# Spreading the next item's first matmuls over the current item's seams, and the routing over the next item's layer 0

## The chip, the cores and the metric

The kernel runs on one core of a Trainium2 chip, with eight items (a batch of 8) worked through one after the other in a single launch. The metric is the device time of one launch in microseconds; the kernel before takes 2810.74 us (median of 3 runs, 2806.79 to 2811.39). The engines are named as the profile names them: PE is TensorE's matmul, PEld its weight load, DVE is VectorE, ACT is ScalarE, POOL is GpSimd, SP is SyncE.

## What is computed

All is fp32. Each item is an image of 256 channels and 1024 positions (tokens). Cut to what matters:

```python
# layer 0: eight heads of width 64, softmax over the QUERY axis
qkv  = xt @ w_qkv + b_qkv
attn = softmax(einsum('bihd,bjhd->bijh', q, k) * SCALE, axis=1)
x    = einsum('bijh,bjhd->bihd', attn, v) @ w_out + b_out + xt
# layer 1
n1 = layer_norm(x)
t  = x + softmax((n1 @ W.T) @ n1.T) @ n1
n2 = layer_norm(t)
# 8 experts, the best 2 per token
probs   = softmax(n2 @ router_w.T)
combine = top 2 of probs, divided by their sum
moe     = n2 + sum over e of combine[:, e] * (gelu(n2 @ w1[e] + b1[e]) @ w2[e] + b2[e])
out     = t + moe
```

## The kernel before

The first seven items go through layer 0, attention and routing; the routing scatters their normalised tokens to memory by expert. The last item's layer 0 is followed by all blocks of the experts, and the last item itself takes all experts in a dense way. One item on the way, in the order of the program:

```python
for b in range(B):
    xT = next_x
    if b + 1 < B:
        next_x = load_x(b + 1)
    t1 = layer0(b, xT)
    if b + 1 < B:
        t2 = attend(b, t1)
        dispatch(b, t2, groups[0])
        continue
    ...   # last item: experts, then attend and dense
```

Layer 0 begins with the values for all heads and the first pair of heads' q and k. `big` is a PSUM tile of 1024 columns, of which there are three buffers; `acc` one of 512 columns, of which there are two, both held by the output `po` all through layer 0.

```python
def project(b, xT, g, t):                      # q (t=0) or k (t=1) of one pair of heads
    pq = big(f"pqk_{b}_{g}_{t}")
    ...                                        # 4 matmuls of 512 columns
    dst = two.tile([P, S], F32, tag=f"qk{t}", ...)
    evicted[b, g, t] = nc.vector.tensor_scalar(dst, pq, b_qk[...], ..., ALU.add, ALU.mult)
    return dst

def values(b, xT):
    v = one.tile([P, NT, INNER], F32, tag="v", name=f"v_{b}")
    for i in range(0, NT, 2):                  # 4 parts of two token blocks
        pv = big(f"pv_{b}_{i}")
        ...                                    # 4 matmuls of 512 columns
        for j in range(2):
            nc.vector.tensor_add(v[:, i + j, :], pv[:, ts(j, 512)], b_v)
    return v

def layer0(b, xT):
    v = values(b, xT)
    res = one.tile([P, NPAIR, S], F32, tag="res", name=f"res_{b}")
    qks = [[project(b, xT, 0, t) for t in range(2)]]
    if b == 0:
        prepare()
    steps = [(g, j) for g in range(NPAIR) for j in range(NT)]    # 4 pairs x 8 blocks
    ...
    for at in range(last + LAG + 1):
        if at <= last:
            score(at, 0, 0)                    # psc: scores, a big buffer per head
        if 0 < at <= last + 1:
            score(at - 1, 1, 1)
            soften(at - 1, 1)                  # DVE maximum, ACT exponential; DVE scales v
        if at <= last:
            first_max(at, 0)                   # DVE maximum of the first half
            score(at, 0, 1)
            score(at, 1, 0)
            soften(at, 0)
            first_max(at, 1)
        if at >= LAG:
            gather_values(at - LAG)            # po: exponentials times values
        if at <= last:
            g, j = steps[at]
            if g + 1 < NPAIR and j in (3, 5):
                ...
                qks[g + 1].append(project(b, xT, g + 1, len(qks[g + 1])))
    ...                                        # pr: output projection and residual into t1
```

Attention normalises, transposes (`pt`, copied to nT), multiplies with W (`px`, copied to xa), and takes the eight blocks of queries in turn, scores of one block ahead of the products of the one before:

```python
def attend(b, t1, step=lambda i: None):
    n1 = one.tile([P, NT, D], F32, tag="n", name=f"n1_{b}")
    layer_norm(t1, n1, 1e-5, f"a{b}")
    nT = ...
    to_channels(n1, nT, f"n1_{b}")             # 16 transposes on PE, two copies on DVE
    ...                                        # px, xa
    def mix(i, ex, ssum):
        pt = big(f"pa_{b}_{i}")
        for m in range(NT):
            nc.tensor.transpose(pt[:, ts(m, P)], ex[:, ts(m, P)], ident)
        aT = two.tile([P, S], F32, tag="tr", name=f"aT_{b}_{i}")
        nc.vector.tensor_copy(aT, pt)
        py = acc(f"py_{b}_{i}")
        ...                                    # 8 matmuls, then rs and the sum into t2
```

`dispatch` then does the second norm, the transposes, the logits on TensorE (`pl`), and the routing, a chain of small VectorE instructions of 64 or 8 elements per partition: gates (softmax and the two largest), then the row of every token in its expert's list (with two small matmuls, `pc` and `pn`, that count over the partitions), then 16 indirect DMAs:

```python
def dispatch(b, t2, group):
    n2 = one.tile([P, NT, D], F32, tag="n", name=f"n2_{b}")
    layer_norm(t2, n2, 1e-5, f"f{b}")
    nT = ...
    to_channels(n2, nT, f"n2_{b}")
    gate, hots = gates(b, nT)                  # pl on PE, then the gates on DVE
    ...
    pc = acc(f"pc_{b}")
    nc.tensor.matmul(pc[:, : NT * E], before, flat, start=True, stop=True)
    pn = acc(f"pn_{b}")
    nc.tensor.matmul(pn[:, : NT * E], ones, flat, start=True, stop=True)
    ...                                        # rows, counts, and per choice: row, exp, at
    for i in range(NT):
        for k in range(2):
            nc.gpsimd.indirect_dma_start(out=view[:, :], ..., in_=n2[:, i, :], in_offset=None)
    nc.gpsimd.tensor_add(t2, t2, n2)
    nc.sync.dma_start(group.sums[group.items.index(b)], t2)
```

The order of the program is not wholly that of an engine: the compiler's scheduler may bring a ready instruction forward when an earlier one waits, as far as buffers are free. Buffers of one kind are given out in the program's order.

Of the kernel before, what the change touches and what calls it, by code (L numbers as in the profile page):

```python
# [10 lines left out]
F32 = mybir.dt.float32  # L11
I32 = mybir.dt.int32
AF = mybir.ActivationFunctionType
ALU = mybir.AluOpType
# [4 lines left out]
def kernel(  # L19
# [266 lines left out]
    def values(b, xT):  # L286
        v = one.tile([P, NT, INNER], F32, tag="v", name=f"v_{b}")
        for i in range(0, NT, 2):
            pv = big(f"pv_{b}_{i}")
            for j in range(2):  # L290
                for cc in range(NCC):
                    nc.tensor.matmul(  # L292
                        pv[:, ts(j, 512)],
                        xT[:, cc, ts(i + j, P)],
# [4 lines left out]
            for j in range(2):  # L299
                nc.vector.tensor_add(v[:, i + j, :], pv[:, ts(j, 512)], b_v)  # L300
        return v

    def layer0(b, xT):
# [4 lines left out]
        v = values(b, xT)  # L308
        res = one.tile([P, NPAIR, S], F32, tag="res", name=f"res_{b}")
        qks = [[project(b, xT, 0, t) for t in range(2)]]  # L310
        if b == 0:
            prepare()
# [81 lines left out]
        for at in range(last + LAG + 1):  # L394
# [13 lines left out]
# [3 lines that stand above are left out]
                    if j == 3:  # L411
                        qks.append([])
                    qks[g + 1].append(project(b, xT, g + 1, len(qks[g + 1])))

# [16 lines left out]
    def attend(b, t1, step=lambda i: None):  # L431
        n1 = one.tile([P, NT, D], F32, tag="n", name=f"n1_{b}")
        layer_norm(t1, n1, 1e-5, f"a{b}")
        nT = one.tile([P, NCC, S], F32, tag="nT", name=f"nT_{b}")
# [35 lines left out]
        def mix(i, ex, ssum):  # L470
            pt = big(f"pa_{b}_{i}")
# [3 lines left out]
            nc.vector.tensor_copy(aT, pt)  # L475
            py = acc(f"py_{b}_{i}")
# [22 lines left out]
    def gates(b, nT):  # L499

        pl = acc(f"pl_{b}")
        for i in range(NT):
            for dc in range(NCC):
# [6 lines left out]
                )  # L510

# [6 lines left out]
        pl3 = pl[:, : NT * E].rearrange("p (i e) -> p i e", e=E)  # L518
        m = col("g_m")
        nc.vector.tensor_reduce(m, pl3, AX.X, ALU.max)  # L520
        p = tmp("g_p")
        nc.vector.tensor_sub(p, pl3, bcast(m, E))
        nc.scalar.activation(p, p, AF.Exp)
        z = col("g_z")
        nc.vector.tensor_reduce(z, p, AX.X, ALU.add)
        nc.vector.reciprocal(z, z)
        nc.vector.tensor_mul(p, p, bcast(z, E))

        def first_of_max(src, tag):
# [3 lines left out]
            nc.vector.tensor_tensor(hot, src, bcast(top, E), ALU.is_equal)  # L533
            nc.vector.tensor_mul(hot, hot, rank)
# [4 lines left out]
        top1, hot1 = first_of_max(p, "g_1")  # L539
        rest = tmp("g_rest")  # L540
        nc.vector.scalar_tensor_tensor(rest, hot1, -2.0, p, ALU.mult, ALU.add)
        top2, hot2 = first_of_max(rest, "g_2")
# [25 lines left out]
    def dispatch(b, t2, group):  # L568

        n2 = one.tile([P, NT, D], F32, tag="n", name=f"n2_{b}")  # L570
        layer_norm(t2, n2, 1e-5, f"f{b}")
        nT = one.tile([P, NCC, S], F32, tag="nT", name=f"n2T_{b}")
        to_channels(n2, nT, f"n2_{b}")
        gate, hots = gates(b, nT)
# [7 lines left out]
        pc = acc(f"pc_{b}")  # L582
        flat = both.rearrange("p i e -> p (i e)")
        nc.tensor.matmul(pc[:, : NT * E], before, flat, start=True, stop=True)
        pn = acc(f"pn_{b}")
# [11 lines left out]
        )  # L597
        rows = tmp("d_rows")
# [474 lines left out]
```

## Time and profile before

| what | number |
|---|---|
| time, median of 3 | 2810.74 us |
| span of the profiled execution | 2745.2 us |
| TensorE busy | 2617.9 us (95%) |
| VectorE busy | 1539.6 us (56%) |
| ScalarE busy | 841.2 us (31%) |
| mean granted TensorE clock | 0.983 |
| q, k projections, 512 matmul records | 233.9 us |
| values, 256 matmul records | 137.5 us |

Busy times overlap, so they don't add up to the span. One fp32 matmul of the program stands as two records in the trace; records are pipelined, and a record can begin before the one ahead of it ends, so the mean of a record can be longer than the distance from one to the next. A line of waits reads: engine, tile and line that waited, what it waited for, total us, number of times, the longest. A line of a table by stage reads: stretch, its length, then for PE, PEld, DVE, ACT and POOL the busy us and the number of instructions, then the granted clock, the DMA's busy share, and GB/s.

### The profile page before, as it was taken

What the parts mean: (1) busy time and instruction counts of PE and PEld (TensorE: products, weight loads), DVE (VectorE), ACT (ScalarE), POOL (GpSimd) and SP (SyncE); (2) the same over time, 40 slices, a digit from 0 to 9 for tenths busy, and PEclk for the clock granted to TensorE, in tenths of its full rate; (3) what the DMA queues carried; (4) which work ended last, traced back from release to release, by engine and by line L of the source; (5) the groups of instructions that cost most, each with busy time, mean ns of one, the idle gap of its engine ahead of it and who ended that gap; (6) DMA issues with size and microseconds to landing.
All of it is one profiled execution on the core that took longest, in us unless ns stands there. A gap on an engine that the chain in (4) does not pass through costs nothing.

```text
span 2745.2 us, 27697 instructions
## 1 busy us (share of the span) xinstructions
PE 2617.9 (95%) x10153; PEld 1378.9 (50%) x10153; DVE 1539.6 (56%) x3667; ACT 841.2 (31%) x1455; POOL 385.7 (14%) x383
## 2 busy tenths in 40 slices
PE   8999899989999999999999999899989999999899
PEld 3345433653356335633464346433653377776566
DVE  4764566456744665466645764566456753334544
ACT  2441155114521443134312541145114521111122
POOL 0000200020000200020002000200020024444652
PEclk9999999999999999999999999999999999999999
DMA  6992100000000000010001000100010135553542
GB/s 232 385 340 47 62 1 1 16 35 12 1 16 16 31 1 16 10 37 1 16 0 46 1 1 16 46 1 1 0 37 10 41 125 180 180 178 103 177 141 97
DMA packets 82512, 182.37 MB, mean 66 GB/s; under 512 B 15016, under 2 KB 24904, under 8 KB 80584
## 3 DMA queue, kind: packets, MB, share of 16 engines
q1 hardware_dynamic: 57368, 118.65, 12.1%
q0 software_dynamic: 25008, 61.95, 7.3%
q8 instruction: 80, 1.31, 0.2%
q14 instruction: 56, 0.46, 0.1%
HBM read 100.49 MB, written 110.90 MB: 77 GB/s over the span
## 4 chain that ended last, share of the span: by engine, by line
PE 83%; issue 8%; DVE 4%; ACT 3%; DMA 0%; POOL 0%; ACTq 0%; SPq 0%; DVEq 0%
PE psc L324 20%; PE po L382 17%; PE pqk L273 8%; PE py L478 8%; PE ps L456 7%; PE pv L292 5%; PE pr L420 4%; PE px L441 2%; PE pdh L950 2%; PE pdy L974 2%; PE pt_n L218 2%; PE pa L473 2%; PE pe L798 1%; PE pl L504 1%; ACT hb L783 1%
## 5 line engine op out<-in xcount | busy, mean ns | idle before, releaser
L357 ACT ACTIVATE ex<-psc,nmax 128x1024 f32<-128x1024 f32 x512 | 565.8, 1109 | 784.8 <-DVE scrap L347 776.7
L324 PE MATMUL psc<-qk,qk 64*128 64x512 f32 x2048 | 581.0, 624 | 16.8 <-DVE qk L281 11.0
L382 PE MATMUL po<-ex,vs 128*64 128x512 f32 x2048 | 495.9, 605 | 6.6 <-DVE vs L366 6.6
L335 DVE TENSOR_REDUCE nmax<-psc 128x1 f32<-128x512 f32 x512 | 351.3, 687 | 155.7 <-PE psc L324 155.5
L324 PEld LDWEIGHTS psc<-qk,qk 64*128 64x128 f32 x2048 | 229.8, 185 | 363.4 <-ACT ex L357 177.2
L347 DVE TENSOR_SCALAR_CACHE_REDUCE scrap<-psc,nmax 128x512 f32<-128x512 f32 x512 | 382.3, 747 | 37.5 <-PE psc L324 8.0
L382 PEld LDWEIGHTS po<-ex,vs 128*64 128x64 f32 x2048 | 124.8, 136 | 346.5 <-issue 182.7
L639 POOL TENSOR_TENSOR t<-t,n 128x2048 f32<-128x2048 f32 x7 | 31.6, 4513 | 1767.0 <-issue 1476.1
L478 PE MATMUL py<-n,aT 128*128 128x256 f32 x1024 | 241.5, 390 | 10.9 <-DVE aT L475 10.9
L456 PE MATMUL ps<-nT,xa 128*128 128x512 f32 x512 | 236.9, 593 | 0.0
L273 PE MATMUL pqk<-xT,wqkv 128*128 128x512 f32 x512 | 233.9, 602 | 0.4
L478 PEld LDWEIGHTS py<-n,aT 128*128 128x128 f32 x1024 | 194.0, 194 | 67.7 <-DVE aT L475 42.5
L281 DVE TENSOR_SCALAR qk<-pqk,b_qk 128x1024 f32<-128x1024 f32 x64 | 82.2, 1284 | 186.7 <-PE pqk L273 186.7
L467 ACT ACTIVATE ex<-ps,nmax 128x1024 f32<-128x1024 f32 x64 | 71.3, 1114 | 333.6 <-DVE nmax L464 325.4
L273 PEld LDWEIGHTS pqk<-xT,wqkv 128*128 128x128 f32 x512 | 93.4, 190 | 141.0 <-issue 99.4
L483 DVE SCALAR_TENSOR_TENSOR t<-py,rs,t 128x256 f32<-128x256 f32 x64 | 31.0, 484 | 230.9 <-PE py L478 230.9
L292 PE MATMUL pv<-wqkv,xT 128*128 128x512 f32 x256 | 137.5, 687 | 9.2 <-ACT wqkv L97 7.3
L798 PE MATMUL pe<-wb,hb 128*128 128x256 f32 x504 | 125.4, 392 | 10.9 <-ACT hb L783 10.8
L456 PEld LDWEIGHTS ps<-nT,xa 128*128 128x128 f32 x512 | 93.4, 190 | 79.0 <-issue 72.7
L632 POOL DMA_INDIRECT rows<-n,d_at x112 | 109.0, 973 | 151.2 <-DVE row L619 119.2
L842 POOL DMA_INDIRECT yk<-y,yat x112 | 112.6, 1005 | 98.5 <-DVE o L869 52.2
L420 PE MATMUL pr<-wo,res 128*128 128x256 f32 x512 | 121.9, 381 | 0.0
(171 smaller groups left out, 2479.3 us busy)
## 6 DMA issues: line engine op xcount, KB each, us to landing
rows<-wb SPq DMA_DIRECT2D x7, 8192.0 KB, 52.0
y<-yb SPq DMA_DIRECT2D x63, 256.0 KB, 2.0
xT<-in_x_dram SPq DMA_DIRECT2D x7, 1024.0 KB, 4.9
sums<-t SPq DMA_DIRECT2D x7, 1024.0 KB, 4.4
o<-sums SPq DMA_DIRECT2D x7, 1024.0 KB, 6.5
out_dram<-oT SPq DMA_DIRECT2D x14, 512.0 KB, 7.9
wpack<-in_L_ffn_w_dram SPq DMA_DIRECT2D x4, 1024.0 KB
wb<-in_L_ffn_w_dram SPq DMA_DIRECT2D x16, 256.0 KB, 5.4
```

Source lines behind the costliest of these rows:

```text
L273: nc.tensor.matmul(pq[:, ts(n, 512)], wqkv[:, cc, t, ts(g, P)], xT[:, cc, ts(n, 512)], start=(cc == 0), stop=(cc == NCC - 1),)
L292: nc.tensor.matmul(pv[:, ts(j, 512)], xT[:, cc, ts(i + j, P)], wqkv[:, cc, 2, :], start=(cc == 0), stop=(cc == NCC - 1),)
L324: mm = nc.tensor.matmul(pss[at, h][:, ts(n, 512)], k[r, ts(j, P)], q[r, ts(n, 512)], start=True, stop=True)
L335: firsts[at, h] = nc.vector.tensor_reduce(nmax, pss[at, h][:, ts(0, 512)], AX.X, ALU.max, negate=True)
L347: nc.vector.tensor_scalar(scrap, ps[:, ts(1, 512)], -1.0, nmaxes.pop((at, h)), ALU.mult, ALU.min, accum_out=nmax,)
L357: nc.scalar.activation(ex, ps, AF.Exp, bias=nmax, scale=1.0, accum_out=sums[at][:, h : h + 1])
L382: nc.tensor.matmul(po[n][h * DK : (h + 1) * DK, :], vs[:, h, :], exs[h][:, ts(n, 512)], start=(j == 0), stop=(j == NT - 1),)
L420: nc.tensor.matmul(pr[:, :C], res[:, g, ts(i, P)], wo[:, g, :], start=(g == 0), stop=False)
L456: nc.tensor.matmul(psc[:, ts(n, 512)], xa[:, ec, ts(i, P)], nT[:, ec, ts(n, 512)], start=(ec == 0), stop=(ec == NCC - 1),)
L478: nc.tensor.matmul(py[:, :D], aT[:, ts(m, P)], n1[:, m, :], start=(m == 0), stop=(m == NT - 1))
L798: nc.tensor.matmul(py[:, ts(r, D)], hT[:, fc, ts(r, P)], wb[:, at + fc * D : at + (fc + 1) * D], start=(fc == 0), stop=(fc == NFC - 1),)
L842: nc.gpsimd.indirect_dma_start(out=yk[:, i, k, :], out_offset=None, in_=self.group.y[:, :], in_offset=bass.IndirectOffsetOnAxis(ap=ats[k][ ...
```

## The change

The next item's values and its first q and k no longer stand at the start of its layer 0. A class `Begin` holds them as pieces, and the current item's attention and second norm call for a piece at named places: one projection after the first norm is written, one part of the values before the last block's transposes, one between these and its products, two parts after the second norm is written, and the second projection after the logits. The first item does all its pieces ahead of the loop; the last item's attention has no pieces to place.

The routing is cut into portions with `yield`; one portion follows each step of the next item's layer 0, held on VectorE behind that step's first maximum of the second head. The logits are copied out of PSUM at once. The two counts share one `big` tile, since the `acc` tiles belong to `po` there. The purpose is to give TensorE work where it waits for VectorE and ScalarE between the stages.

```diff
+    class Begin:
+        def values(self, part): ...            # one of the 4 parts: 4 matmuls, 2 adds on DVE
+        def project(self): ...                 # first t=0, then t=1
+        def at(self, place):
+            if place == "norm 1":
+                self.project()
+            elif place == "last weights":
+                self.values(0)
+            elif place == "last products":
+                self.values(1)
+            elif place == "norm 2":
+                self.values(2)
+                self.values(3)
+            elif place == "logits":
+                self.project()
@@ layer0
-    def layer0(b, xT):
-        v = values(b, xT)
+    def layer0(b, xT, begun, routing):
+        v, qks = begun.v, begun.qks
-        qks = [[project(b, xT, 0, t) for t in range(2)]]
-        if b == 0:
-            prepare()
...
                     qks[g + 1].append(project(b, xT, g + 1, len(qks[g + 1])))
+                with tc.issue_after(firsts[at, 1].ins):
+                    next(routing, None)
+        for _ in routing:
+            pass
@@ attend
         layer_norm(t1, n1, 1e-5, f"a{b}")
+        fill("norm 1")
...
         def mix(i, ex, ssum):
+            if i == NT - 1:
+                fill("last weights")
             pt = big(f"pa_{b}_{i}")
...
             nc.vector.tensor_copy(aT, pt)
+            if i == NT - 1:
+                fill("last products")
@@ logits, gates
+        l = small.tile([P, NT, E], F32, tag="g_l", name=f"g_l_{b}", bufs=1)
+        nc.vector.tensor_copy(l.rearrange("p i e -> p (i e)"), pl[:, : NT * E])
...                                            # seven yields inside the gates and behind them
@@ normed, dispatch
+        layer_norm(t2, n2, 1e-5, f"f{b}")
+        fill("norm 2")
+        to_channels(n2, nT, f"n2_{b}")
+        nc.gpsimd.tensor_add(t2, t2, n2)
+        l = logits(b, nT)
+        fill("logits")
...
-        pc = acc(f"pc_{b}")
+        pcn = big(f"pcn_{b}")
+        pc, pn = pcn[:, :512], pcn[:, 512:]
-        pn = acc(f"pn_{b}")
...                                            # five yields in the rest
@@ the loop over items
+    begun = Begin(0, next_x)
+    begun.all()
+    prepare()
+    routing = iter(())
...
-        t1 = layer0(b, xT)
+        t1 = layer0(b, xT, begun, routing)
         if b + 1 < B:
-            t2 = attend(b, t1)
-            dispatch(b, t2, groups[0])
+            begun = Begin(b + 1, next_x)
+            t2 = attend(b, t1, begun.at)
+            n2, _, l = normed(b, t2, begun.at)
+            nc.sync.dma_start(groups[0].sums[b], t2)
+            routing = dispatch(b, n2, l, groups[0])
             continue
```

## The prediction

> **What bounds the kernel now.** I read the page first, then TensorE's waits over the middle items, then one seam between two items (items 3 and 4) by stages, then the instructions in it. The page:
>
> ```profile
> PE 2617.9 (95%) x10153; PEld 1378.9 (50%) x10153; DVE 1539.6 (56%) x3667; ACT 841.2 (31%) x1455; POOL 385.7 (14%) x383
> ...
> PEclk9999999999999999999999999999999999999999
> ...
> PE 83%; issue 8%; DVE 4%; ACT 3%; DMA 0%; POOL 0%; ACTq 0%; SPq 0%; DVEq 0%
> ```
>
> TensorE is busy 95% of the span and makes up 83% of the chain that ended last. DMA has no share in that chain, so only TensorE's holes and slow stretches can be won. TensorE's waits, items 1 to 6 (us in total, times, longest):
>
> ```profile
> PE pt_n L218 <- DVE n L209: 29.8, 12, 2.5
> PE pa L473 <- ACT ex L467: 13.2, 12, 1.7
> PE py L478 <- DVE aT L475: 8.4, 6, 1.4
> PE psc L324 <- DVE qk L281: 6.9, 5, 1.4
> PE po L382 <- DVE vs L366: 5.4, 6, 0.9
> ```
>
> The same holes return once per item: 2.48 us before the transposes of each of two layer norms, 1.74 us before the last transposes of the attention weights, 1.40 us before its last products, and 1.38 us before the next item's first scores. That is about 9.5 us of idle TensorE per item. The stages of one item (busy us by engine, clock, DMA):
>
> ```profile
> 1155.20:1188.80 33.60, 29.81 (x100) 15.23 (x100) 20.88 (x65) 1.75 (x3) 11.15 (x8) 0.95 0.15 55
> 1188.80:1342.90 154.10, 152.57 (x560) 53.03 (x560) 105.91 (x262) 77.28 (x135) 8.91 (x10) 1.00 0.03 9
> ...
> 1360.70:1374.80 14.10, 11.59 (x32) 5.99 (x33) 7.75 (x16) 0.21 (x1) 0.00 (x0) 0.88 0.22 74
> 1374.80:1438.30 63.50, 59.90 (x242) 39.48 (x240) 28.83 (x46) 12.20 (x18) 0.00 (x0) 1.00 0.00 1
> ```
>
> In order: from the end of attention to the first scores (33.6 us), layer 0's steps (154.1), norm 1 and the projection after it (14.1), attention (63.5). Layer 0 has no TensorE hole worth having. The first and third also run at a clock of 0.95 and 0.88: 33.6 x 0.05 = 1.7 us and 14.1 x 0.12 = 1.7 us lost. In the timeline the weight loads of the values stand 0.85 us apart just after the hole and 0.43 us later.
>
> **What the Trainium skill says.** "TensorE: Matmul & The Clock Gate", Why this matters for your kernels, wants no TensorE gaps over about 3 us, and Part 1 of that page has the clock halve after idling. The trace agrees on the half (0.85 against 0.43 us); here a gap of 2.5 us is already followed by slow matmuls. "Perfetto Trace Analysis", Identifying the Most-Contended Engine, calls matmul busy time a poor measure of headroom; that bears on the 95%, which contains slow matmuls and transposes that trickle behind VectorE. "VectorE: DVE Perf Modes", The TRN2 errata, gives (N+151)/0.96 ns for an fp32 tensor_tensor: 224 ns for the routing's 64 elements; the trace has 218 to 225. So the routing's cost is its number of instructions. "Perfetto Trace Analysis", Optimization Strategy, reads repeated bubbles as a possible lack of PSUM or SBUF. No wait in layer 0 shows one before; the change could make one, below.
>
> **Part 1: filling the holes (7 seams).** A projection is 8 matmul records at 0.43 us, 3.44 us; its row over the kernel agrees (x512 in 64 projections). A part of the values is also 8 records, 3.44 us, so a seam moves 4 x 3.44 + 2 x 3.44 = 20.6 us of TensorE work out of layer 0's head.
>
> Norm 1 takes one projection. Before, the stage lasts 14.1 us. After: 3.44 us of projection, during which the norm's eight writes (0.335 apart, 2.67 us in all) run; then I put the projection's eviction (1.28 us) ahead of the two copies of nT (1.22 each), so px starts 0.7 us later than before, but warm: 16 x 0.43 = 6.9 instead of 7.6 us. The stage stays at about 14.1 us and 3.4 us of work has gone in free. **Saved: 3.4.**
>
> The last block takes two parts of the values, 6.9 us, across holes of 1.74 and 1.40 us. **Saved: 3.1**; the other 3.8 us are only moved.
>
> Norm 2 to first scores was 33.6 us; 3.4 + 6.9 = 10.3 us have left it, so 23.3 us would be no gain. After: values 2 and 3, 6.9 us, covering the norm's chain (0.48 + 0.43 + 0.18 + 0.17 + 0.21 + 0.20 us, then writes); 16 transposes at their own pace, 2.0 us (eight of the attention's take 1.04); logits 3.4 us (30 records in 3.46); projection 3.4, about half of it slipping in before the logits while VectorE makes nT; and the wait of 1.4 us for that projection's eviction, which stays. Sum 17.1 to 17.2. **Saved: 6.1.**
>
> Together 3.4 + 3.1 + 6.1 = 12.6 us per seam. It may be checked against the other side: holes 9.5 + clock 3.4 + trickling transposes about 3 (two norms at 4.0 and 3.2 us against 2.0 each) = 15.9 us were there to be won, and 12.6 leaves the eviction wait and some of norm 1.
>
> **Part 2: routing in layer 0.** It used to lie beside the values and cost TensorE little. Counted from the code and the rows: 21 VectorE instructions for the gates and 19 for the rows, 8.4 us busy, some 9.5 us with 0.03 us between them, in 13 portions, one after each of layer 0's first 13 steps. What room a step has (two plain steps, and one with a projection):
>
> ```profile
> 1329.39:1333.41 4.02, 4.02 (x18) 1.40 (x17) 3.23 (x10) 2.45 (x5) 0.00 (x0) 1.00 0.00 0
> 1333.41:1337.28 3.87, 3.87 (x19) 1.27 (x17) 2.94 (x8) 2.15 (x5) 0.00 (x0) 1.00 0.01 2
> 1202.70:1210.70 8.00, 7.99 (x25) 2.89 (x24) 4.60 (x12) 2.66 (x5) 0.00 (x0) 1.00 0.01 2
> ```
>
> VectorE is idle 0.8 to 0.9 us in a plain step, in one piece of 0.63 to 0.78 us waiting for scores: just where a portion falls. In a step with a projection it has over 3 us (steps 3, 5 and 11 of the 13). Portions of 0.4 to 0.75 us fit. Over 0.7 are portion 6 (0.95 us), 7 (0.8 plus some 0.7 us to TensorE and back), 8 and 9 (1.0 each); I count 0.05 + 0.25 + 0.8 + 0.3 + 0.3 = 1.7 us through to TensorE, because scores, maximum, exponential and the release of the PSUM buffer make a tight ring. In steps 7 and 8 the two counts also take one of the three big PSUM buffers that the scores rotate through, for about one step; with two left, the next score must await an exponential (1.1 us), and I put 1.5 us on it. **Cost: 3.2 per seam.**
>
> Net 12.6 - 3.2 = 9.4 us, times 7 seams = 66 us. Item 0's start, the experts and the last item's attention have no fillers and stay. From 2810.7 that gives **2745 us**. The profiled execution (span 2745.2) is 64 us shorter than the median of the timed ones; I don't know why, and take the difference in us over unscaled.
>
> **Rivals.** *A: the routing's delays outweigh.* If each of the ten portions in plain steps delays the ring by its whole length (some 8 us) and the PSUM buffer costs two steps' overlap (3 us), 11 of the 12.6 us are lost: 12.6 - 11 = 1.6, times 7 = 11 us, about 2800. For it: the ring has almost no TensorE slack, each step's score weight loads wait on the exponential (PEld psc <- ACT ex). Against: the 0.63 us hole of VectorE sits at the right place, and project steps swallow a 1.28 us eviction with psc growing only from 2.0 to 2.57 us. *B: the fillers displace the chains that they should hide.* VectorE now evicts values (0.69 each) in the norms; if two evictions go ahead of each norm's writes and TensorE waits for them, each seam loses some 3 us of the gain: 6.4 x 7 = 45 us, 2766. For it: VectorE executes in a fixed order. Against: in norm 2 TensorE has 6.9 us of other work. *C: it goes better than counted.* The projection slips into the 0.90 us hole before layer 0's last products, the logits' projection hides its own eviction, and routing costs nothing: 12.6 + 0.9 + 1.4 = 14.9, times 7 = 104 us, 2707.
>
> **Range and chances.** A has perhaps one chance in five in a strong form, B one in four, and C one in six. I take 2715 to 2785 as the range. 2% is 56 us, so faster than 2754.5 needs 8.0 us net per seam; the estimate of 9.4 is only a little better, hence 0.62 for faster by over 2%, 0.34 within 2%, and 0.04 slower by over 2%, which would need several steps to go wrong at once.
>
> **What would show it.** Right: pt_n <- n and psc <- qk almost gone from TensorE's waits, clock near 1.0 in the seam, end of attention to first scores about 17 us, the period from first scores to first scores down from 286.7 to about 277 us, layer 0's steps 154 to about 157. Wrong in part 2: layer 0 over 160 us, with po or psc waiting on VectorE or ACT in steps 0 to 12. Wrong in part 1: pt_n or px waiting for copies behind v or qk evictions. The prediction as a whole fails if the time between score groups in those 13 steps grows by more than half a microsecond each.

## The result and the profile after

The changed kernel takes 2742.53 us (median of 4 runs, 2739.48 to 2745.55) against 2808.76 us for the kernel before in the same session (4 runs, 2804.14 to 2811.39): a ratio of 0.9766, 95% interval 0.9748 to 0.9784, or 66 us less. The prediction said 2745. The total fits; the way to it fits only in part, and this is the use of what follows.

The page of the changed kernel, its lines of busy time, clock and chain:

```profile
PE 2627.3 (96%) x10153; PEld 1382.2 (50%) x10153; DVE 1530.7 (56%) x3675; ACT 840.3 (31%) x1455; POOL 388.4 (14%) x383
...
PEclk9999999999999999999999999899999999999899
...
PE 85%; issue 7%; DVE 4%; ACT 2%; DMA 1%; another core or an unknown queue 0%; ACTq 0%; SPq 0%; DVEq 0%; POOL 0%
```

TensorE has the same 10153 matmul records as before, yet is busy 9.4 us longer (2627.3 against 2617.9), though the kernel is faster. Matmuls have grown longer somewhere: busy time here is no measure of TensorE's speed. TensorE's waits over items 1 to 6, to just behind item 7's first scores (total, times, longest):

```profile
PE pt_n L218 <- DVE n L209: 11.6, 6, 1.9
PE psc L360 <- DVE qk L281: 8.3, 6, 1.4
PE px L482 <- DVE nT L219: 7.2, 6, 1.2
PE psc L360 <- ACT ex L393: 6.7, 7, 1.7
```

The waits of 29.8, 13.2, 8.4 and 5.4 us are gone or shrunk; one pt_n wait per item is left, in norm 1, and the wait for the eviction ahead of the first scores stayed: the prediction's sum had kept it, its list of signs had it almost gone. Two waits are new or longer: 1.2 us per item ahead of px, and up to 1.7 us for the exponential ahead of scores (0.4 before). The stages of one seam and item, in order: end of attention to first scores, first scores to first products, the rest of layer 0's steps, and norm 1 after the output projection.

```profile
1143.90:1162.50 18.60, 17.22 (x75) 10.09 (x73) 10.39 (x21) 0.21 (x1) 4.54 (x1) 0.88 0.14 56
1162.50:1175.10 12.60, 12.59 (x23) 5.53 (x23) 7.12 (x20) 5.57 (x9) 0.00 (x0) 0.50 0.00 0
1175.10:1324.40 149.30, 148.27 (x545) 50.68 (x544) 104.23 (x282) 73.09 (x129) 15.52 (x16) 1.00 0.04 15
...
1342.05:1357.40 15.35, 12.21 (x39) 5.60 (x38) 8.85 (x17) 0.21 (x1) 0.00 (x0) 1.00 0.21 68
```

The second row is new: TensorE is busy for all of 12.6 us at a clock of 0.50. The same stretch of the kernel before was 8.15 us at 1.00.

The table below cuts every traced kernel in the same way; each entry is the mean over items 1 to 6, from TensorE's timeline, in us. The column "layer 0" is from the first products to the output projection. Read it across first, then down.

| kernel | first scores to products | layer 0 | norm 1 and px | attention | its end to next first scores | item |
|---|---|---|---|---|---|---|
| before, the profile shown at the start | 8.15 | 145.85 | 14.08 | 67.18 | 35.24 | 288.15 |
| before, traced again (e1) | 8.14 | 153.39 | 13.55 | 67.19 | 34.91 | 294.83 |
| after | 12.45 | 149.24 | 15.39 | 70.54 | 17.92 | 283.18 |
| after, traced again (e8) | 12.02 | 149.19 | 15.39 | 70.54 | 18.32 | 283.11 |
| routing only (e4) | 9.93 | 148.97 | 13.71 | 67.19 | 36.16 | 293.61 |
| fillers only (e3; e10) | 10.30; 10.30 | 154.97; 154.80 | 16.77; 15.92 | 70.55; 70.54 | 22.02; 22.01 | 292.27; 291.24 |
| fillers, scatter late (e5; e11) | 10.24; 10.21 | 145.95; 152.73 | 16.46; 16.49 | 70.55; 70.55 | 22.53; 22.48 | 283.39; 290.12 |
| dense after the logits (e2) | 9.51 | 149.17 | 16.63 | 70.55 | 15.95 | 279.46 |
| e2 and norm 1's eviction last (e6) | 10.58 | 149.34 | 13.37 | 70.55 | 16.00 | 277.50 |
| e2 and counts copied at once (e7) | 10.46 | 147.44 | 16.02 | 70.55 | 16.22 | 278.33 |
| all three (e9) | 9.62 | 147.25 | 13.37 | 70.54 | 15.97 | 274.41 |
| e9 with a projection more after the logits (e12) | 9.39 | 147.27 | 13.37 | 69.69 | 19.08 | 276.45 |

The first two rows are one and the same kernel. Their difference, 7.5 us per item in layer 0, is the second half of the story.

### The profile page after: what moved, and what is told of

It is laid out like the page before. It is cut to its first block, busy times and chain, and to the rows that moved or that the text cites. A ratio compares the mean times of both kernels' runs of the same rounds, so it can differ in the third digit from the quotient of the medians.

```text
span 2741.3 us, 27690 instructions
## 1 busy us (share of the span) xinstructions
PE 2627.3 (96%) x10153; PEld 1382.2 (50%) x10153; DVE 1530.7 (56%) x3675; ACT 840.3 (31%) x1455; POOL 388.4 (14%) x383
## 4 chain that ended last, share of the span: by engine, by line
PE 85%; issue 7%; DVE 4%; ACT 2%; DMA 1%; another core or an unknown queue 0%; ACTq 0%; SPq 0%; DVEq 0%; POOL 0%
PE psc L360 21%; PE po L418 17%; PE pqk L273 9%; PE py L523 8%; PE ps L497 7%; PE pr L460 4%; PE pv L304 4%; PE pdy L1040 2%; PE pe L863 2%; PE px L482 2%; PE pdh L1016 2%; PE pa L516 2%; PE ph L838 2%; PE pl L549 1%; PE pt_n L218 1%
## 5 line engine op out<-in xcount | busy, mean ns | idle before, releaser
L360 PE MATMUL psc<-qk,qk 64*128 64x512 f32 x2048 | 613.4, 655 | 21.1 <-DVE qk L281 11.0
L418 PE MATMUL po<-ex,vs 128*64 128x512 f32 x2048 | 505.0, 607 | 0.3 <-DVE vs L402 0.3
L360 PEld LDWEIGHTS psc<-qk,qk 64*128 64x128 f32 x2048 | 244.1, 194 | 378.4 <-ACT ex L393 174.0
L273 PE MATMUL pqk<-xT,wqkv 128*128 128x512 f32 x512 | 243.2, 612 | 0.5
L281 DVE TENSOR_SCALAR qk<-pqk,b_qk 128x1024 f32<-128x1024 f32 x64 | 82.1, 1283 | 165.2 <-PE pqk L273 160.1
L304 PE MATMUL pv<-wqkv,xT 128*128 128x512 f32 x256 | 117.4, 602 | 9.0 <-ACT wqkv L97 7.1
```

The costliest lines, as they stand in the source:

```text
L273: nc.tensor.matmul(pq[:, ts(n, 512)], wqkv[:, cc, t, ts(g, P)], xT[:, cc, ts(n, 512)], start=(cc == 0), stop=(cc == NCC - 1),)
L304: nc.tensor.matmul(pv[:, ts(j, 512)], self.xT[:, cc, ts(i + j, P)], wqkv[:, cc, 2, :], start=(cc == 0), stop=(cc == NCC - 1),)
L360: mm = nc.tensor.matmul(pss[at, h][:, ts(n, 512)], k[r, ts(j, P)], q[r, ts(n, 512)], start=True, stop=True)
L418: nc.tensor.matmul(po[n][h * DK : (h + 1) * DK, :], vs[:, h, :], exs[h][:, ts(n, 512)], start=(j == 0), stop=(j == NT - 1),)
```

## The experiments

The kernel before does not take the same time on every chip: its median was 2745.82 us on one (7 runs), 2824.95 on another (25 runs), 2814.68 on a third (8 runs). They are called chips A, B and C below. Each was used in one session only, so what belongs to the chip and what to the session can't be told apart. The chip of the first profile is not on record; its 2746.91 us fit A. Each ratio is the record's, against the kernel before on the same chip; it is not exactly the quotient of the two medians.

| run | chip | us | ratio and 95% interval |
|---|---|---|---|
| e1, before again | B | 2828.04 | 1.0002, 0.9979 to 1.0024 |
| e2, dense after the logits | B | 2719.98 | 0.9628, 0.9598 to 0.9657 |
| e3, fillers only | B | 2806.23 | 0.9931, 0.9906 to 0.9955 |
| e4, routing only | B | 2816.28 | 0.9954, 0.9934 to 0.9974 |
| e8, after again | A | 2716.84 | 0.9894, 0.9878 to 0.9911 |
| e5, fillers, scatter late | A | 2715.07 | 0.9889, 0.9872 to 0.9905 |
| e6, norm 1's eviction last | A | 2672.78 | 0.9733, 0.9717 to 0.9749 |
| e7, counts copied at once | A | 2679.15 | 0.9765, 0.9746 to 0.9785 |
| e9, all three | C | 2682.11 | 0.9530, 0.9509 to 0.9550 |
| e12, a projection more after the logits | C | 2694.42 | 0.9568, 0.9546 to 0.9590 |
| e10, fillers only again | C | 2798.56 | 0.9945, 0.9910 to 0.9981 |
| e11, scatter late again | C | 2791.61 | 0.9918, 0.9895 to 0.9941 |

The theories in short. For the seam: the changed kernel loses to a cold clock and to an eviction in the wrong place what the fillers win there; the rival is that the routing's delays eat it. For the 66 us as a whole: the seams give only about half, and the rest are holes of VectorE beside the scatter that the new placement removes; the rival is that the fillers alone give it all.

### e1: the kernel before, traced again

No edit. The profile taken before the prediction had a span of 2745.2 us, the timed runs 2804 to 2811. What is longer in them?

> The kernel before, unchanged. Its profile on record has a span of 2745 us, its timed runs 2804 to 2811 us, so 64 us of the timed runs are in no trace yet. Theory S (the last item's stretch, after its layer 0, [...]has stalls that come and go): the new trace is near 2810 us, its items 0 to 6 keep a period of 287 to 290 us, and the 64 us lie after 2170 us. Rival R (all of the kernel is a little slower when timed, a matter of clock): the period of the items is some 2% longer, about 294 us, and the tail grows in proportion.

Measured: a span of 2827.1 us. Layer 0 of item 0, which has no scatter beside it, takes 145.9 us here as in the first profile; layer 0 of items 1 to 6 takes 153.4, of item 7 156.4 (148.0 there). A further 29 us lie behind the last item's px: from there to the end 272.7 us instead of 243.7. The other stages agree within 0.6 us in the mean; only item 0's way to the next first scores differs more (37.0 against 32.2; over the items of the two traces it varies from 32 to 37). The holes stand where the scatter's 16 indirect DMAs end. Timeline of the kernel before traced again, GpSimd, VectorE and TensorE (start, length, instruction, idle time and releaser):

```profile
929.54 0.97 POOL L632 DMA_INDIRECT rows<-n,d_at  x1 [0.30 <-issue]
...
930.97 0.69 DVE L335 TENSOR_REDUCE nmax<-psc 128x1 f32<-128x512 f32 x1 [3.50 <-PE psc L324]
...
933.08 0.75 DVE L347 TENSOR_SCALAR_CACHE_REDUCE scrap<-psc,nmax 128x512 f32<-128x512 f32 x1 [1.42 <-remote]
...
935.19 2.07 PE L324 MATMUL psc<-qk,qk 64*128 64x512 f32 x2 [4.28 <-ACT ex L357]
```

VectorE stands idle for 3.50 us, then for 1.42 with a releaser that the profile can't name ("remote"); ScalarE and TensorE starve behind it. The hole is paid twice, since the clock falls after it (same kernel, by stretches):

```profile
932.00:936.00 4.00, 0.81 (x1) 0.50 (x2) 2.89 (x8) 1.20 (x2) 0.00 (x0) 0.78 0.00 0
936.00:940.00 4.00, 4.00 (x10) 0.77 (x8) 1.82 (x5) 2.30 (x4) 0.00 (x0) 0.50 0.01 2
```

Theory S fails: the items' period is 294.8 us, not 287 to 290, and only 29 of the 82 us lie behind the last layer 0. Rival R has the period right, but not its cause, since item 0's layer 0 is no longer than before. So the prediction was worked out on a trace that is 64 us shorter than its session's timed runs and 82 us shorter than this one.

### e8: the changed kernel on chip A

No edit; on the chip where the kernel before shows no holes.

> The changed kernel, unchanged, as the reference for its variants on the same chip: near 2742 us, ratio to the kernel before between 0.965 and 0.98. The medians of its stages in the trace repeat: norm 1 near 15.4 us, first scores to first products near 12.5, then 149.4 to the output projection.

Measured: 0.9894, outside the expected ratio: 29 us less, not 66. Its items take 283.11 us, as in the first trace of the changed kernel (283.18). In the stage means the two traces of the changed kernel differ by less than half a microsecond; behind the last px they differ by 29, 243.6 us here and 272.5 there, as the kernel before does. So the changed kernel has no holes in layer 0 on either chip, and the change as such is worth about 30 us. It can be summed from the traces: item 0 8.0 us shorter, items 1 to 6 each 5.0 us shorter (288.15 - 283.11), the last item 7.8 us longer, as it has the routing's cost and the slow first scores and no fillers, and the way to item 0's first scores 0.2 us longer: 8.0 + 30.2 - 7.8 - 0.2 = 30.2 us, which is the difference of the spans, 2745.2 - 2715.0.

### e3 and e10: the fillers without the spread routing

```diff
-            routing = dispatch(b, n2, l, groups[0])
+            for _ in dispatch(b, n2, l, groups[0]):
+                pass
```

> The changed kernel with the routing done at once, ahead of the next item's layer 0, and not in portions: part 1 of the change alone. If portions are what makes the fillers pay: some 9.5 us of VectorE's small instructions stand before or among the first scores of each item, 5 to 8 us per seam longer, 2778 to 2798 us. If the routing's cost is only the PSUM buffer of the two counts (3.2 us per seam in the changed kernel's trace): within 1% of 2742 us.

> The fillers-only kernel (routing at once, scatter at the start of layer 0) as the partner of the next run on the same chip. On a chip with the long holes in VectorE (kernel before near 2825 us): layer 0 from first products at 154.8 us and about 2806 us, as before. On a chip without them (kernel before near 2746 us): layer 0 at 146 us, and 2715 to 2725 us.

Measured: 0.9931 on B and 0.9945 on C, only 16 to 19 us less. Layer 0 lasts 155 us: the holes of the kernel before are all there, some larger. VectorE in e3, two holes at the end of the scatter:

```profile
1215.12 0.69 DVE L371 TENSOR_REDUCE nmax<-psc 128x1 f32<-128x512 f32 x1 [3.31 <-remote]
...
1222.23 1.28 DVE L281 TENSOR_SCALAR qk<-pqk,b_qk 128x1024 f32<-128x1024 f32 x1 [6.02 <-remote]
```

The last of the 16 DMAs was issued at 1218.63. Of the second hole some 3.2 us are not new: VectorE waits as long for a projection without any hole (3.15 and 3.21 us in e6's item 0). e3's total lies outside both expected ranges. The rival for the total is out: the fillers alone don't give 66 us on a chip with holes. A second thing shows in e3's TensorE, ahead of the first scores:

```profile
1194.81 0.66 PE L650 MATMUL pcn<-d_both,before 128*128 128x64 f32 x2 [5.21 <-DVE d_both L646]
```

With the values gone from here, nothing covers the routing's chain any longer: TensorE waits 5.21 us for it, and the way to the first scores is 22.0 us instead of the changed kernel's 17.9.

### e4: the spread routing without the fillers

```diff
+        if b > 0:
+            begun = Begin(b, xT)
+            begun.all()
         t1 = layer0(b, xT, begun, routing)
         if b + 1 < B:
-            begun = Begin(b + 1, next_x)
-            t2 = attend(b, t1, begun.at)
-            n2, _, l = normed(b, t2, begun.at)
+            t2 = attend(b, t1, nothing)
+            n2, _, l = normed(b, t2, nothing)
```

> The changed kernel with all values and both projections back at the head of each item's layer 0, the routing still in portions: part 2 of the change alone. By the prediction's terms it costs 3.2 us per seam against the kernel before, less some 2 us for the two counts and the slow values that leave the head: 2809 + 7 x 1 = 2816 us, between 2800 and 2830. If the whole gain came from the tail of the last item and not from the seams, it would be near 2743 us like the changed kernel.

Measured: 0.9954 (by the medians 8.7 us less). Layer 0 takes 148.97 us, and no hole is in it, though the chip is B. Against item 0 of the same run, whose layer 0 has neither routing nor scatter (145.91 us), the routing costs 3.1 us there. So two things happen at once in layer 0: the routing's portions cost 3.1 us, and 7.5 us of holes go away.

The routing also costs something in the first scores, 9.93 us instead of 8.14, although here the values and both projections stand right ahead of them and the clock is 1.00 when they start:

```profile
1207.90:1217.80 9.90, 8.16 (x22) 3.37 (x22) 6.70 (x20) 5.13 (x9) 0.00 (x0) 0.83 0.00 0
1213.33 4.56 PE L360 MATMUL psc<-qk,qk 64*128 64x512 f32 x10 [1.71 <-ACT ex L393]
```

In the kernel before, that wait for the first exponential is 0.43 us; now a table load stands in front of it (see e2). So the routing's new place costs 3.1 + 1.8 = 4.9 us per item.

On B the two parts alone shorten an item by 2.6 and 1.2 us (292.27 and 293.61 against 294.83); the whole change has items 11.7 us shorter than the kernel before on B. Most of what is missing, 5.4 of 7.9 us, lies in the head of the seam, where with the fillers alone the routing's chain stands open (e3).

### e5 and e11: the routing at once, only the scatter late

This is e3 with the last two casts and the 16 DMAs held to step 12 of the next layer 0.

```diff
-            for _ in dispatch(b, n2, l, groups[0]):
+            whole = dispatch(b, n2, l, groups[0])
+            while next(whole) != "scatter":
                 pass
+            def wait(rest):
+                for _ in range(12):
+                    yield
+                yield from rest
+            routing = wait(whole)
```

> Fillers as in the changed kernel, the routing at once ahead of layer 0 as in the fillers-only run, but its last two casts and so the 16 scatter DMAs held until step 12 of layer 0. Theory P (VectorE's long unexplained holes in layer 0 come with the scatter standing in the first 20 us of layer 0; the portions as such do nothing): layer 0 from first products to output projection falls from 154.8 us to 146 to 148, no hole with an unknown releaser, some 7 us per seam, 2755 us. Rival (the holes come from the lump of routing or from the fillers): layer 0 stays at 154 to 155 us and the total at 2800 us; or the hole moves along with the scatter to step 12 and beyond.

> The same with the scatter held until step 12. On a chip without the holes it can differ from its partner only by small amounts, within 5 us. On a chip with them: theory P (the holes come with the scatter in the first steps) layer 0 at 146 to 148 us and 2755 us against 2806; rival: no difference, or the holes move along to step 12.

Measured: e5 came to chip A, which has no holes to move, and takes 2715.07 us, as the changed kernel there (2716.84). That settles something else: without holes, spreading the routing buys nothing over doing it at once with a late scatter. The head of the seam shrinks by 4.2 us (22.53 to 18.32), layer 0 grows by 3.2, the first scores by 1.8, and norm 1, which varies, shrinks by 1.1. e11 on C was to say whether the holes belong to the first 20 us of layer 0. They don't: they moved along with the scatter to step 12. By stretches, e11:

```profile
684.00:688.00 4.00, 3.25 (x16) 0.98 (x12) 0.74 (x2) 0.08 (x1) 3.07 (x4) 1.00 0.28 98
...
692.00:696.00 4.00, 3.53 (x10) 0.77 (x8) 2.58 (x7) 0.20 (x1) 0.00 (x0) 0.50 0.09 33
```

VectorE (third number pair) does 0.74 us of work in 4, while POOL issues the last DMAs (671.72 to 690.83). My theory, that the place early in layer 0 makes the holes, fell. What does separate the kernels with holes from those without is how the DMAs are issued. In the kernel before, e3, e5, e10 and e11 all 16 follow each other 1.27 us apart, 19.1 us from the first start to the last. In all others one choice's indices are cast two portions earlier, and the DMAs come in two runs of eight. GpSimd in the changed kernel:

```profile
945.54 0.97 POOL L700 DMA_INDIRECT rows<-n,d_at  x1 [0.30 <-issue]
948.26 0.97 POOL L700 DMA_INDIRECT rows<-n,d_at  x1 [1.75 <-DVE d_at L694]
```

Eight start from 936.60 to 945.54, eight from 948.26 to 957.18. Layer 0 was free of holes in every trace with two runs of eight (eight traces on all chips), and had them in every trace with sixteen on chips B and C; the two traces with sixteen and no holes are e5 on A and the first profile of the kernel before. That is an agreement, not a proof: the length of the run was not varied by itself, since all eight also have the routing in portions, and what VectorE waits for is not named by any view. The Trainium skill, "SBUF — State Buffer", SBUF: two separate sides, describes a port pair that VectorE and GpSimd take exclusively, VectorE in a two-port mode or with two SBUF inputs. The instructions behind the holes shown here read their tensor from PSUM, so that passage does not by itself account for them, nor would it say why one chip is spared. No run here tests it.

### e2: dense matmuls after the logits

Of the pieces in the seam, the last part of the values goes behind the logits, and the second projection ahead of them.

```diff
             elif place == "norm 2":
                 self.values(2)
-                self.values(3)
-            elif place == "logits":
                 self.project()
+            elif place == "logits":
+                self.values(3)
```

> The changed kernel with two pieces exchanged: the second projection (k) runs after norm 2, the last part of the values after the logits. Theory C (in the changed kernel TensorE's clock halves because the 128x8 logits, the eviction wait of 1.4 us and the first scores follow each other with no dense matmul between): the clock at the first scores is near 1.0, the 22 first score records take 8 us instead of 12.6, the wait for k's eviction is gone, some 6 us less per seam, 7 seams: 2700 us. Rival (the slow first scores come from the routing or from VectorE, not from the clock): they stay at 12 us and only the wait of 1.4 us goes, 7 times: 2733 us.

Measured: items of 279.46 us instead of 283.2, a gain of 3.7 us and not of 6. First the changed kernel's TensorE around its logits:

```profile
1155.37 3.83 PE L549 MATMUL pl<-rT,n2T 128*128 128x8 f32 x30
1159.05 2.06 PE L273 MATMUL pqk<-xT,wqkv 128*128 128x512 f32 x2
1162.48 12.69 PE L360 MATMUL psc<-qk,qk 64*128 64x512 f32 x22 [1.38 <-DVE qk L281]
```

The logits are 30 records that stream 8 columns each: 3.8 us of "busy" TensorE with next to nothing to do. Behind them two records of the projection already take 2.06 us (two of them ahead of the logits took 1.02), then comes a wait of 1.38 us, then the scores, 64 rows deep and paced by VectorE and ScalarE. In the clock, 1158 to 1161 us has 0.53, 1161 to 1173 has 0.50, and only from 1176 it is 1.00 again. Now e2, same stretch, then its stages (end of attention to first scores, first scores to first products):

```profile
1147.89 3.41 PE L549 MATMUL pl<-rT,n2T 128*128 128x8 f32 x30
1151.16 1.10 PE L304 MATMUL pv<-wqkv,xT 128*128 128x512 f32 x2
1152.19 3.70 PE L360 MATMUL psc<-qk,qk 64*128 64x512 f32 x12
```

```profile
1136.40:1152.20 15.80, 15.80 (x74) 9.48 (x72) 9.11 (x19) 0.21 (x1) 4.53 (x1) 1.00 0.16 66
1152.20:1161.10 8.90, 7.09 (x25) 3.12 (x24) 7.78 (x22) 5.14 (x9) 0.00 (x0) 1.00 0.00 0
```

The scores start at once, since the eviction of k was done during the values, and the clock stays at 1.00; 8.9 us instead of 12.6. In this seam only two records of the values stand behind the logits, as in the changed kernel only two of the projection did: the scheduler drew the others forward. In two of e2's six items (9.84 and 11.67 us) part of the loss comes back, and in e6 and e7, which keep e2's order, more of it (means 10.58 and 10.46).

The clock's changes suggest why. In each of the 14 traces it is 1.00 or 0.50, the stretches at 0.50 begin on one grid with a step of 3.41 us, and they last whole steps, but for the one at the trace's end. In the seam of the changed kernel shown above it falls at 1158.18, while the logits still run and ahead of the wait, and rises at 1175.25, five steps later. What a seam does goes with where on this grid its block of 30 logit records begins. From 1.13 to 1.41 us behind a grid point, all five such seams in the two traces of the changed kernel fall and need 12.35 to 12.48 us to the first products; all six in e2 and e7 stay at 1.00 and need 8.9. From 0.60 to 1.08 us, both orders fall (e2, e6 and e7: 11.67 to 12.62 us). So e2's order removes the fall at some positions and not at others, and a seam's position shifts with the length of the items. That is an agreement over these seams; the position was not set by itself. Whether it is the dense records or the missing wait that helps was not varied apart.

The Trainium skill, "TensorE: Matmul & The Clock Gate", HAM oscillation — how this bites in real kernels, describes a clock that halves over and over when TensorE waits between bursts of matmuls; the trace agrees on the half, and shows it setting in during matmuls that count as busy.

A smaller loss of the same stage: ScalarE's table load for the exponentials, 1.28 us, used to fall to the routing's exponential in the seam and now falls to layer 0's first one (changed kernel, groups of ScalarE):

```profile
L393 ACT ACT_TABLE_LOAD x7 | 9.0, 1283 | 145.1 <-DVE scrap L383 145.1
```

The Trainium skill, "ScalarE: Activation LUTs", What ACT_TABLE_LOAD costs, has the same 1283 ns. It stands right behind VectorE's row maximum, on the path to the first products: TensorE's wait for that exponential is 1.81 us in e2's seam and 0.43 in the kernel before. That fits the 8.9 us that the best items keep where 8.15 was; no run moved the load away.

### e6: norm 1's eviction behind the norm's own chain

e2, and the q eviction of the filler in norm 1 is held on VectorE until the second copy of nT is issued.

```diff
             if place == "norm 1":
-                self.project()
+                self.pq = multiply(self.b, self.xT, 0, 0)
+            elif place == "channels 1":
+                self.qks[0].append(evict(self.b, 0, 0, self.pq))
...
-        to_channels(n1, nT, f"n1_{b}")
+        copied = to_channels(n1, nT, f"n1_{b}")
+        with tc.issue_after(copied.ins):
+            fill("channels 1")
```

> The kernel with dense work after the logits (2720 us), with one thing more: at norm 1 the eviction of the projection is held on VectorE behind the second copy of nT. Theory: in the changed kernel this eviction (1.28 us, after a wait of 1.27 us for TensorE) stood ahead of the reciprocal and the norm's eight writes, and so made the transposes 1.9 us late and let the clock drop in some items. Then norm 1 falls from 15.4 to 17.8 us to about 13 us, 2.4 to 5 us per seam, 2695 to 2703 us. Rival (TensorE is not what sets this stage's end, or the held eviction makes the scores wait for the PSUM buffer): within 5 us of 2720.

Measured: norm 1 in 13.37 us, 2.0 less than in the changed kernel and 3.3 less than e2's mean. The changed kernel's norm 1, where the eviction (qk) came first:

```profile
1344.72 1.28 DVE L281 TENSOR_SCALAR qk<-pqk,b_qk 128x1024 f32<-128x1024 f32 x1 [1.27 <-PE pqk L273]
1345.92 0.19 DVE L207 RECIPROCAL rstd_a<-rstd_a 128x8 f32<-128x8 f32 x1
...
1346.61 2.70 PE L218 MATMUL pt_n<-ident,n 128*128 128x128 f32 x16 [1.93 <-DVE n L209]
```

VectorE first waits 1.27 us for the filler itself and then spends 1.28 us on it; the reciprocal, ready long before, stands behind both, and TensorE waits 1.93 us for n: the filler delays the chain it was to hide. In e6 the same eviction comes after the copies:

```profile
1321.20 0.20 DVE L207 RECIPROCAL rstd_a<-rstd_a 128x8 f32<-128x8 f32 x1 [0.27 <-ACT rstd_a L206]
1321.61 2.67 DVE L209 TENSOR_SCALAR n<-t,mv_a,rstd_a 128x256 f32<-128x256 f32 x8 [0.20 <-DVE rstd_a L207]
1324.70 2.36 DVE L219 COPY nT<-pt_n 128x1024 f32<-128x1024 f32 x2 [0.42 <-PE pt_n L218]
1326.97 1.27 DVE L287 TENSOR_SCALAR qk<-pqk,b_qk 128x1024 f32<-128x1024 f32 x1
```

On chip A, e6, which has e2's edit too, takes 44.1 us less than the changed kernel (2716.84 to 2672.78). Its items are only 2.0 us shorter than e2's, since its first scores are 1.1 us longer.

### e7: the counts leave PSUM at once

e2, and `pc` is copied out of the shared PSUM tile in the portion that reads `pn`, so that the buffer goes back to the scores' rotation a step earlier.

```diff
+        ahead = tmp("d_ahead")
+        nc.vector.tensor_copy(ahead.rearrange("p i e -> p (i e)"), pc[:, : NT * E])
...
-        nc.vector.tensor_add(
-            rows, rows, pc[:, : NT * E].rearrange("p (i e) -> p i e", e=E)
-        )
+        nc.vector.tensor_add(rows, rows, ahead)
```

> The kernel with dense work after the logits (2720 us), with the second count copied out of the shared PSUM tile in the portion that makes it, so that the big buffer is free one portion earlier. Theory: holding the third big buffer over a step is a part of the routing's 3.2 us in steps 6 to 9; 1 to 2 us per seam come back: 2706 to 2713 us. Rival (the cost is the matmuls' wait for VectorE and the extra buffer as such): within 3 us of 2720, or a little longer by the added copy.

Measured: layer 0 in 147.44 us instead of 149.17, so the held buffer costs 1.7 us of the routing's 3.3, for one more VectorE instruction.

### e9 and e12: the three together, and one step too far

e9 is e6 with e7's edit. e12 asks whether still more dense work behind the logits helps:

```diff
             elif place == "last weights":
                 self.values(0)
-            elif place == "last products":
-                self.values(1)
             elif place == "norm 2":
+                self.values(1)
                 self.values(2)
-                self.project()
             elif place == "logits":
+                self.project()
                 self.values(3)
```

> Both steps together: dense work after the logits, norm 1's eviction held behind the copies of nT, and the second count copied out at once. Alone, the two last gave 2672.8 and 2679.2 us on a chip where the kernel before takes 2745.8. If they add (norm 1 at 13.4 us, layer 0 from first products at 147.5 us): 2672.8 - 7 x 1.8 = 2660 us there, ratio to the kernel before 0.969; on a chip where the kernel before takes 2825 us, 2690 to 2700 us. If the earlier release only moves the wait: 2672 us, ratio 0.973.

> As the combined kernel, but twice the dense work after the logits: the last products get no piece, norm 2 takes values 1 and 2, and after the logits stand the second projection and values 3, some 6.9 us. Theory C (the clock at the first scores depends on dense matmuls behind the sparse logits): first scores to first products falls from about 10 us, with 12 in some items, to 8.2 us in all items, and the clock is 1.0 there; against it the hole of 1.4 us before the last products comes back: together 0 to 2.5 us less per seam, 0 to 17 us in all. Rival (3.4 us of dense work are enough, and what is left has other causes): first scores as in the combined kernel, and the time some 10 us longer by the hole.

Measured: e9 0.9530, the best of all, with items of 274.41 us. The gains add as expected: norm 1 takes 13.37 us and layer 0 147.25. The granted clock is 0.989 (0.973 in the changed kernel). Its page, against the 2627.3 us of busy TensorE in the changed kernel:

```profile
PE 2580.4 (96%) x10153; PEld 1361.3 (51%) x10153; DVE 1527.2 (57%) x3682; ACT 840.7 (31%) x1455; POOL 389.3 (15%) x383
```

The same 10153 records in 46.9 us less. e12 is 12.3 us slower than e9 on the same chip: the first scores gain 0.2 us, attention 0.85, but in every second item the head of the seam takes 20.76 us. A second dense piece behind the logits does not pay: the first scores take 8.89 to 9.99 us and not 8.2, and the hole ahead of the last products is open again.

## Why the prediction was right, and where it was not

**The total: right by luck, since two errors cancel.** That the profiled execution is 64 us shorter than the timed ones, a difference taken "in us over unscaled", hid them. From the trace the prediction expected 66 us; on a chip like the traced one the change gives 29 us (e8). On the record's chip it gives 66, because the holes beside the scatter go too. They can't have gone by the fillers (e3, e10 keep them) and they do go with the routing's new place (e4). No trace of the kernel before on the record's chip exists, so the remaining 66 - 29 = 37 us is a difference and not a sum. It fits: there the kernel before takes 63 us more than on A, and 29 us behind the last px stay in the changed kernel, which leaves 34 us for seven layers, some 5 us each; on B it is 7.5 to 8.4 each.

**Part 1, filling the holes, 12.6 us per seam: the sum right, partly by luck.** By term: the head of the seam was to save 6.1 beyond the 10.3 us moved out, and shrank by 17.3 (35.24 to 17.92), so 7.0. The last block was to save 3.1: attention grew by 3.4 for 6.9 us of work, so 3.5. Norm 1 was to save 3.4: it grew by 1.3, so 2.1. Sum 12.6. The head's 7.0 owe something to the reference: the prediction read one of the short seams, 33.6 us where the mean is 35.24; it expected the head to end at 17.2 us, and it takes 17.92.

**Norm 1: wrong in its order.** "I put the projection's eviction (1.28 us) ahead of the two copies of nT" was still too late in the queue: it stood ahead of the reciprocal and all eight writes. That is rival B, in one stage out of three, 1.3 us against the kernel before and 2.0 against what e6 reaches. In norm 2, where TensorE had 6.9 us of other work, B did not happen.

**Part 2, routing, 3.2 us: right where it looked, with one term missing.** Layer 0 grew by 3.4 us (145.85 to 149.24), in e4 by 3.1. The PSUM buffer was put at 1.5; e7 recovers 1.7. Rival A did not happen. Not foreseen were the 1.8 us in the first scores (e4), where the table load now stands: 4.9 us in all, in e4.

**What was missing: the first scores, 4.3 us per item.** The prediction put the end of the seam at the first scores and took what follows as unchanged. First scores to first products went from 8.15 to 12.45 us. The seams of e2 that stay at a clock of 1.00 need 8.9 us with the same routing and table load, so some 0.75 us are theirs and 3.5 go with the clock. Part of these may be the table load's too, since in e4 the clock falls to 0.50 behind the 1.71 us of waiting for it. The step that failed is a reading, "the weight loads of the values stand 0.85 us apart just after the hole". In the seam that was read they stand behind the logits:

```profile
1162.65 3.46 PE L504 MATMUL pl<-rT,n2T 128*128 128x8 f32 x30
1167.10:1170.50 3.40, 3.40 (x5) 1.35 (x4) 1.80 (x6) 0.00 (x0) 0.00 (x0) 0.50 0.19 77
```

The hole ahead of the transposes ended at 1157.65, and the clock was still 1.00 while the logits ran. In norm 1, and in three of the second norms, a fall does follow the hole itself. But six of the seven seams have one that begins at the logits' end (from 2.2 us ahead of it to 1.1 behind), and the dense values that stood there paid for it. The prediction charged this to the hole, which the fillers would remove, and moved away the work that had been paying. That the fall now lands on the first scores is shown (12.6 us at 0.50); that the fillers brought it there and not the routing follows from e4, whose scores start at 1.00, and e2, which moves fillers alone.

So 12.6 - 3.4 - 4.3 = 4.9 us per seam instead of 9.4. Of the prediction's own signs the way to the first scores (about 17 us) came true. The period, 283.2 us and not 277, the clock in the seam, 0.88 and 0.50, and the steps of layer 0, 12.45 + 149.24 = 161.7 us and not 157, did not; "layer 0 over 160 us" struck, only in part for the routing that it was meant to catch.

**Rival C** can't be read off the changed kernel; but its idea, that the projection could hide its own eviction, is e2, and with e6 and e7 the seam comes to 288.15 - 274.41 = 13.7 us, near its 14.9, though by other terms: the routing still costs 1.4 us in layer 0, and the first scores 1.5.

## What to carry to other kernels

Order the fillers of a seam by what they leave behind: an operand that needs an eviction goes early, and work that fills TensorE goes last, behind any sparse matmuls, so that the next stage can start at full clock and without a wait (here it did so in part of the items). Take the stage behind the seam into the sum: the work that is moved away may have been paying for something that stays, here a clock that falls behind the logits and a table load. A filler's own eviction is queued on the engine whose chain the filler hides; hold it behind that chain explicitly. And before summing stages from a trace, compare its span with the timed median: if they differ by more than the effect sought, the trace lacks something the change may touch.

## What the hardware showed that I had not expected

- The same kernel takes 2746, 2815 or 2825 us on three chips (or in three sessions), at mean clocks of 0.983 (first profile) and 0.970 (e1). The difference traced is VectorE's holes beside and after a run of 16 indirect DMAs, 7.5 us per layer 0, and 29 us behind the last item's px. The latter is in the changed kernel as well (243.6 and 272.5 us) and was not looked into.
- The clock fell to 0.50 while TensorE counted as busy: at 1158.18, inside 3.8 us of matmuls that stream 8 columns each. It stayed there for 17.1 us, through a wait of 1.4 us and the 64-row scores paced by VectorE. Its stretches at 0.50 are whole steps of 3.41 us on one grid per trace, and the same order of instructions gave 8.89 us in one seam and 12.62 in another (e7).
- Splitting the 16 DMAs into two runs of eight, 2.7 us from start to start, goes with no holes in layer 0 on the chips that had them. Whether the pause is the cause stays open; the direct test, the kernel before with a pause after the eighth DMA, was not made.
